# Side chains that no longer stand behind each other in the queues, and a maximum spread in float32r: a Perceiver block on one core

## The chip, the core and the metric

The kernel runs on one core of one Trainium2 chip. The metric is the device time in microseconds (us) from one launch. Three runs of the kernel before took 2706.93, 2708.26 and 2709.93 us; the median is 2708.26 us. One further execution was profiled: it took 2710.54 us, and 2708.8 us of that lie between its first and its last instruction (its span).

Five instruction streams matter. TensorE (PE) does the matmuls, with a weight load ahead of each. VectorE (DVE) and ScalarE (ACT) do elementwise work, GpSimd (POOL) as well, and SyncE (SP) issues the DMAs. Each takes its instructions in the order in which they were built into the program, so an instruction that waits holds up all behind it on its engine.

## The reference

The input is `x`, 8 batches of 64 rows by 512, and a context of 8 batches of 1601 rows by 512. Six residual blocks follow each other:

```python
x = x + L0_xattn(layernorm(x), ctx)   # 32 heads of 128, 8 key/value heads, softmax over 1601 keys
x = x + L0_attn(layernorm(x))         # Mamba: conv, selective scan over 64 steps, 1024 channels, 16 states
x = x + L0_ffn(layernorm(x))          # ternary 512 x 512
x = x + L1_xattn(layernorm(x), ctx)   # no weights: softmax(x ctx^T) ctx
x = x + L1_attn(layernorm(x))         # 32 heads of 16, rotary, causal, 64 tokens
x = x + L1_ffn(layernorm(x))          # octonion gate/up/down, ternary, hidden 1360
```

All is float32. The first block is by far the largest: keys and values are projected from the whole context for each of 8 batches and 8 key/value heads. The change touches its softmax in one place and the order of the five later blocks in another.

## The kernel before

**Attention.** `x_all` (L527) walks over 64 units, one for each batch and key/value head. A unit projects keys (`x_k`, matmuls on L363) and values (`x_v`, L334), forms scores with keys on the partitions (`x_s`, L385), copies them to SBUF (L388) and keeps a running maximum over the key tiles on DVE (L392). In the next unit's six steps the previous unit's softmax is finished: `x_max` (L397) transposes the running maximum (L403) and reduces it to one negative maximum per query, a column `mc` of 128 x 2 (L405). `x_spread` (L408) then spreads that column over all partitions: two matmuls on L412 whose stationary operand is the column broadcast to 128 x 128 and whose moving operand is the identity. DVE adds the result to the scores (L426), ACT takes the exponent (L427), POOL sums over key tiles (L429, L452), PE multiplies by the values (L464), and `x_wo` (L521) applies the output projection. Projections and scores are split in float32r high and low parts, three matmuls for each product; a float32 matmul is recorded as two.

**Side work.** While PE is occupied by the attention, other work is mixed in. `prep` (L616) splits and ternarizes the weights of the later blocks. `chain` (L779) does the five later blocks for a group of two batches: `mamba`, the small `ffn`, `xattn1`, `attn1`, `ffn1`. Groups 0 to 2 get a chain each while the attention of later batches runs; they are called chains 0, 1 and 2 here. Chain 3, for the last two batches, can only start when the attention is over, and this last stretch of the program is called the tail. All are Python generators. `run` (L1303) advances them whenever the attention yields, each at a pace set by a cost and an end (`advance`, L1331), so that prep and chain 0, chains 0 and 1, and chains 1 and 2 are in progress together for part of the time.

**Order.** A scheduler orders the traced instructions on each engine by its own timing model and the data dependences. It may move side work ahead of attention work that was traced before it. To hold it back, the chains see DVE, ACT and POOL through a wrapper (`Late`, L55; `Side`, L68). Every instruction issued through it gets an ordering edge, with no semaphore, to the instruction traced just before it on the same engine:

```python
return lambda *a, **k: self.tc.keep_in_program_order(f(*a, **k))
```

That predecessor may belong to the attention, to the same chain, or to another chain or prep. Instructions on PE and SP are not held. The wrapper is switched off (`pinning`) once the attention's last unit is traced; chain 3 is never held. In the profile all held instructions carry line L65, that of the lambda.

The four stages of the scan in `mamba` (L895) alternate between POOL, DVE, POOL and DVE. `xattn1` (L1015) streams the context again from memory for its scores (L1039) and values (L1095). In the profile, chains 0 to 2 read the context there into a tile named `b` with a left operand also named `b` (`acc<-b,b`); the rows of chain 3 name `s` in its place.

Of the kernel before, what the change touches and what calls it, by code (L numbers as in the profile page):

```python
# [9 lines left out]
FR = mybir.dt.float32r  # L10
# [6 lines left out]
P = 128  # L17
# [37 lines left out]
class Late:  # L55


    def __init__(self, kernel, eng):
        self.kernel, self.tc, self.eng = kernel, kernel.tc, eng

    def __getattr__(self, name):
        f = getattr(self.eng, name)
        if not self.kernel.pinning:
            return f
        return lambda *a, **k: self.tc.keep_in_program_order(f(*a, **k))  # L65


class Side:  # L68


    def __init__(self, kernel, engines):
        self.nc = kernel.tc.nc
        self.late = {e: Late(kernel, getattr(self.nc, e)) for e in engines}

    def __getattr__(self, name):
        return self.late.get(name) or getattr(self.nc, name)
# [2 lines left out]
class Kernel:  # L79
    def __init__(self, ctx, tc, ins, out):  # L80
        self.ctx, self.tc, self.nc = ctx, tc, tc.nc
        self.i = ins
        self.out = out
        self.B = ins["x"].shape[0] // T
        self.n = 0
        self.pinning = True
        self.flush = False

    def nm(self, s):
        self.n += 1  # L90
        return f"{s}_{self.n}"
# [55 lines left out]
    def consts(self):  # L147
        nc, i = self.nc, self.i
        c = self.ctx.enter_context(self.tc.tile_pool(name="const", bufs=1))
        self.c = c  # L150
        self.ident = c.tile([P, P], FP, name="ident")
        make_identity(nc, self.ident)
        self.eps5 = c.tile([P, 1], FP, name="eps5")
        nc.gpsimd.memset(self.eps5, 1e-5)
        self.ones = c.tile([P, P], FP, name="ones")
        nc.gpsimd.memset(self.ones, 1.0)
        self.eps6 = c.tile([P, 1], FP, name="eps6")
        nc.gpsimd.memset(self.eps6, 1e-6)

        def ld(name, shape):  # L160
            t = c.tile(shape, FP, name="c_" + name)
            nc.sync.dma_start(out=t, in_=i[name])
            return t

        self.bq = ld("bq", [P, 32])
        self.bk = ld("bk", [P, NKV])
        self.bv = ld("bv", [P, NKV])
# [229 lines left out]
    def x_max(self, b, i):  # L397

        nc = self.nc
        m = self.mf.pop((b, i))  # L400
        ps = self.px.tile([P, 2, 256], FP, name=self.nm("m_ps"), tag="m", bufs=MB)
        for h in range(2):
            nc.tensor.transpose(ps[:, 0, h * P : (h + 1) * P], m[:, 0, h * P : (h + 1) * P], self.ident)  # L403
        col = self.sb("mc", [P, 2], pool=self.xp, bufs=2)
        nc.vector.tensor_reduce(col, ps[:, 0].rearrange("p (h k) -> p h k", k=P), AX.X, ALU.max, negate=True)  # L405
        self.mm[(b, i)] = (ps, col)

    def x_spread(self, b, i):  # L408

        ps, col = self.mm[(b, i)]  # L410
        for h in range(2):
            self.nc.tensor.matmul(  # L412
                ps[:, 1, h * P : (h + 1) * P], lhsT=col[:, h : h + 1].to_broadcast([P, P]), rhs=self.ident, start=True, stop=True
            )

    def x_exp(self, b, i, n):
# [1086 lines left out]
```

## Time and profile before

| | before |
|---|---|
| median of three runs | 2708.26 us |
| profiled execution, and its span | 2710.54 us, 2708.8 us |
| PE busy | 2569.9 us, 95% |
| DVE, ACT, POOL busy | 1670.9, 1354.6, 1253.5 us |
| DMA | 455.59 MB, mean 168 GB/s |
| last attention instruction on PE ends | 2404.3 us |
| the two spread matmuls, L412 | 256 PE records, mean 283 ns |
| mean granted TensorE clock | 0.977 |

The busy times are unions of the recorded spans. PE's records overlap, since the next matmul starts while the last drains; what a matmul occupies is better read from the space between one start and the next. The chain of waits follows, from the last instruction back, what released each step.

### The profile page before, as it was taken

To read this page: it belongs to the slowest core of one execution; us is meant where nothing else is said; L and a number is where in the kernel's file an instruction comes from. 1 tells how busy PE (TensorE), PEld (TensorE's weight loads), DVE (VectorE), ACT (ScalarE), POOL (GpSimd) and SP (SyncE) were. 2 spreads that over 40 slices of the span, in tenths; PEclk is the share of its full clock that TensorE was granted. 3 is DMA by queue.
4 is the path that set the end of the run, shared out by engine and by line. 5 is a ranking of instruction groups with operands and counts; after the bars stand their busy time and mean duration, and the time that the engine had idled before them with its cause. 6 is when DMAs were issued, how large, how long until landed. Compare 5 with 4: busy or idle time off the path is not lost.

```text
span 2708.8 us, 43887 instructions
## 1 busy us (share of the span) xinstructions
PE 2569.9 (95%) x16288; PEld 2274.8 (84%) x16288; DVE 1670.9 (62%) x2723; ACT 1354.6 (50%) x3128; POOL 1253.5 (46%) x1243
## 2 busy tenths in 40 slices
PE   7999999999999899999999999999999999977787
PEld 6999999889899799978988988988898888964545
DVE  4444345577687865545577676554657777668744
ACT  4444554444566554544455545544546545446443
POOL 3212434464589864422358457521239556405410
PEclk9999999999999999999999999999999999987898
DMA  9544446665666235655234543665343454476764
GB/s 309 153 141 155 137 144 227 200 209 179 212 215 204 71 117 164 210 185 172 88 110 135 157 148 101 206 197 173 101 133 91 137 162 151 141 236 216 233 234 174
DMA packets 302934, 455.59 MB, mean 168 GB/s; under 512 B 80248, under 2 KB 179576, under 8 KB 298240
## 3 DMA queue, kind: packets, MB, share of 16 engines
q1 hardware_dynamic: 302720, 452.79, 52.2%
q8 instruction: 128, 2.10, 0.3%
q14 instruction: 86, 0.70, 0.1%
HBM read 380.23 MB, written 72.48 MB: 167 GB/s over the span
## 4 chain that ended last, share of the span: by engine, by line
PE 67%; DVE 10%; POOL 9%; DMA 7%; issue 4%; ACT 3%; SPq 0%; POOLq 0%; DVEq 0%; ACTq 0%
PE v_ps L334 15%; PE k_ps L363 15%; PE o_ps L464 10%; PE s_ps L385 8%; POOL a L65 4%; DVE a L65 3%; PE w_ps L521 3%; PE acc L274 3%; PE acc L819 2%; PE acc L1095 2%; POOL ss L452 2%; PE acc L1039 2%; PE acc L774 1%; PE acc L777 1%; DMA d_wo<-b 1%
## 5 line engine op out<-in xcount | busy, mean ns | idle before, releaser
L363 PE MATMUL k_ps<-cxb,wk 128*128 128x384 f32 x2304 | 469.9, 347 | 32.1 <-DVE mx L392 16.8
L334 PE MATMUL v_ps<-wv,cxb 128*128 128x256 f32 x3456 | 471.0, 283 | 1.4 <-DVE mx L392 1.2
L334 PEld LDWEIGHTS v_ps<-wv,cxb 128*128 128x128 f32 x3456 | 439.2, 189 | 22.0 <-issue 14.0
L363 PEld LDWEIGHTS k_ps<-cxb,wk 128*128 128x128 f32 x2304 | 405.2, 191 | 50.2 <-DVE mx L392 19.8
L464 PE MATMUL o_ps<-S,v 128*128 128x256 f32 (+1 forms) x1664 | 413.3, 381 | 6.0 <-DVE rw L479 3.9
L385 PE MATMUL s_ps<-q,kt 128*128 128x256 f32 (+1 forms) x2496 | 413.7, 299 | 5.2 <-DVE kt L109 3.1
L388 ACT COPY S<-s_ps 128x512 f32<-128x512 f32 (+1 forms) x448 | 242.4, 553 | 250.0 <-PE s_ps L385 246.9
L385 PEld LDWEIGHTS s_ps<-q,kt 128*128 128x128 f32 (+1 forms) x2496 | 342.1, 185 | 28.0 <-issue 6.9
L452 POOL TENSOR_TENSOR ss<-ss,S 128x512 f32<-128x512 f32 x254 | 353.7, 1392 | 14.6 <-ACT S L427 1.5
L429 POOL TENSOR_TENSOR ss<-S,S 128x512 f32<-128x512 f32 x64 | 85.0, 1328 | 586.9 <-ACT S L427 586.6
L392 DVE TENSOR_TENSOR mx<-s_ps,mx 128x512 f32<-128x512 f32 x256 | 175.4, 685 | 289.5 <-ACT S L388 288.8
L464 PEld LDWEIGHTS o_ps<-S,v 128*128 128x128 f32 (+1 forms) x1664 | 299.5, 190 | 45.0 <-issue 5.7
L108 ACT ACTIVATE kt<-k_ps,c_bk 128x384 fp32r<-128x384 f32 (+1 forms) x256 | 152.0, 594 | 240.7 <-PE k_ps L363 239.6
L426 DVE TENSOR_TENSOR S<-S,m_ps 128x512 f32<-128x512 f32 (+1 forms) x448 | 257.3, 641 | 24.4 <-PE m_ps L412 23.9
L427 ACT ACTIVATE S<-S 128x512 f32<-128x512 f32 (+1 forms) x448 | 247.4, 599 | 44.4 <-DVE S L426 43.8
L109 DVE SCALAR_TENSOR_TENSOR kt<-k_ps,c_bk,kt 128x384 fp32r<-128x384 f32 (+1 forms) x256 | 161.0, 629 | 170.9 <-ACT kt L108 169.4
L337 ACT COPY v<-v_ps 128x256 f32<-128x256 f32 (+1 forms) x416 | 152.7, 369 | 198.1 <-PE v_ps L334 195.7
L334 PE MATMUL v_ps<-wv,cxt 128*128 128x256 f32 (+1 forms) x1536 | 213.2, 286 | 2.7 <-DVE kt L109 1.6
L334 PEld LDWEIGHTS v_ps<-wv,cxt 128*128 128x128 f32 (+1 forms) x1536 | 195.3, 176 | 15.5 <-issue 6.5
L65 DVE TENSOR_TENSOR_SCAN a<-a,a 128x512 f32<-128x512 f32 x96 | 156.1, 1629 | 65.4 <-POOL a L65 65.4
L363 PE MATMUL k_ps<-cxt,wk 128*128 128x450 f32 x768 | 181.1, 378 | 0.9 <-DVE mx L392 0.8
L65 ACT ACTIVATE a<-lv,c_A_log 128x128 f32<-128x128 f32 x384 | 123.0, 394 | 105.3 <-DVE a L65 103.8
(358 smaller groups left out, 3971.3 us busy)
## 6 DMA issues: line engine op xcount, KB each, us to landing
wo<-d_wo SPq DMA_DIRECT2D x96, 512.0 KB, 5.0
wk<-d_wk SPq DMA_DIRECT2D x63, 512.0 KB, 3.8
wv<-d_wv SPq DMA_DIRECT2D x31, 1024.0 KB, 5.6
cst<-in_ctxT_dram SPq DMA_DIRECT2D x96, 192.0 KB, 3.1
b<-in_ctxN_dram SPq DMA_DIRECT2D x36, 512.0 KB, 3.9
d_q<-q_t SPq DMA_DIRECT2D x32, 512.0 KB, 4.4
q<-d_q SPq DMA_DIRECT2D x64, 256.0 KB, 3.5
d_wo<-b SPq DMA_DIRECT2D x32, 512.0 KB, 3.1
```

The costliest lines, as they stand in the source:

```text
L65: return lambda *a, **k: self.tc.keep_in_program_order(f(*a, **k))
L109: eng.scalar_tensor_tensor(lo, src, bias, hi.bitcast(FP), ALU.add, ALU.subtract)
L334: nc.tensor.matmul(ps[:r], lhsT=cx[:, a, c, o : o + r], rhs=w[:, m, c, :], start=k == 0, stop=k == 11)
L337: nc.scalar.copy(vt[:r], ps[:r])
L363: nc.tensor.matmul(ps[:, :wd], lhsT=w[:, a, c, :], rhs=cx[:, m, c, :], start=k == 0, stop=k == 11)
L385: nc.tensor.matmul(sp[:r, gi, :], lhsT=kt[:, a, o : o + r], rhs=q[:, m, :], start=k == 0, stop=k == 2)
L388: nc.scalar.copy(s[:r, :n], sp[:r, :n])
L392: nc.vector.tensor_tensor(mx, sp, S[0] if len(S) == 1 else mx, ALU.max)
L426: nc.vector.tensor_tensor(sv, sv, ps[:r, 1:2].to_broadcast([r, w, 256]), ALU.add)
L427: nc.scalar.activation(sv, sv, AF.Exp, scale=ISC)
L452: nc.gpsimd.tensor_tensor(ss, ss, S[n], ALU.add)
L464: nc.tensor.matmul(ps[:, 0], lhsT=self.v[(b, j, t)][:r, hc : hc + P], rhs=S[t // 2][:r, t % 2], start=t == 0, stop=t == NT - 1)
```

## The change

Two things change.

First, the wrapper gets an owner. Prep and each chain have a number, and every held instruction is noted under its number. A held instruction is now tied to the last instruction on its engine that belongs to the attention (no owner noted) or to its own chain; instructions of other chains and of prep are skipped in that search.

Second, the column `mc` becomes float32r, and the moving operand of the spread is a float32r copy of the identity, made once by ACT.

```diff
 class Late:
-    def __init__(self, kernel, eng):
-        self.kernel, self.tc, self.eng = kernel, kernel.tc, eng
+    def __init__(self, kernel, eng, own):
+        self.kernel, self.tc, self.eng, self.own = kernel, kernel.tc, eng, own
+
+    def pin(self, made):
+        owner = self.kernel.owner
+        ins = made.ins
+        for i in reversed(self.tc.nc.cur_bb.bb.instructions):
+            if i is not ins and i.engine == ins.engine and owner.get(i.name, self.own) == self.own:
+                dep = mybir.DependencyInfo(mybir.DependencyClass.NoSync, mybir.DependencyReason.DATA)
+                self.tc.add_manual_dep(ins, i.name, dep, reason="side")
+                break
+        owner[ins.name] = self.own
+        return made
 
     def __getattr__(self, name):
...
-        return lambda *a, **k: self.tc.keep_in_program_order(f(*a, **k))
+        return lambda *a, **k: self.pin(f(*a, **k))
...
 class Side:
     def __init__(self, kernel, engines):
         self.nc = kernel.tc.nc
-        self.late = {e: Late(kernel, getattr(self.nc, e)) for e in engines}
+        kernel.sides += 1
+        self.late = {e: Late(kernel, getattr(self.nc, e), kernel.sides) for e in engines}
...
+        self.sides, self.owner = 0, {}
...
+        self.ident_r = c.tile([P, P], FR, name="ident_r")
+        nc.scalar.copy(self.ident_r, self.ident)
...
-        col = self.sb("mc", [P, 2], pool=self.xp, bufs=2)
+        col = self.sb("mc", [P, 2], FR, pool=self.xp, bufs=2)
...
-                ps[:, 1, h * P : (h + 1) * P], lhsT=col[:, h : h + 1].to_broadcast([P, P]), rhs=self.ident, start=True, stop=True
+                ps[:, 1, h * P : (h + 1) * P], lhsT=col[:, h : h + 1].to_broadcast([P, P]), rhs=self.ident_r, start=True, stop=True
```

## The prediction

> **What bounds the kernel now.** I read the page first, then stretches of the span, the groups of instructions, the chain of waits in order of time, and the timeline around one spread.
>
> ```profile
> span 2708.8 us, 43887 instructions
> PE 2569.9 (95%) x16288; PEld 2274.8 (84%) x16288; DVE 1670.9 (62%) x2723; ACT 1354.6 (50%) x3128; POOL 1253.5 (46%) x1243
> PE   7999999999999899999999999999999999977787
> PEclk9999999999999999999999999999999999987898
> ```
>
> PE is busy throughout, except for the last five of 40 slices: the tail, from 2404 to 2709 us. Stretches show where PE still idles under the attention, and which engine is then loaded (the columns: length, then PE, weight loads, DVE, ACT and POOL busy, granted clock, DMA share, GB/s):
>
> ```profile
> 1400.00:1500.00 100.00, 98.01 (x681) 87.62 (x679) 74.64 (x111) 56.35 (x134) 72.09 (x70) 1.00 0.41 121
> 2100.00:2200.00 100.00, 97.08 (x621) 89.92 (x620) 73.01 (x106) 51.30 (x126) 53.30 (x57) 0.99 0.45 140
> 2200.00:2300.00 100.00, 94.10 (x595) 85.90 (x593) 73.53 (x94) 51.42 (x131) 63.10 (x70) 1.00 0.51 162
> 2300.00:2404.00 104.00, 93.44 (x561) 84.53 (x562) 64.49 (x111) 45.28 (x109) 36.67 (x37) 0.95 0.45 147
> 2404.00:2553.00 149.00, 114.81 (x670) 81.14 (x668) 119.37 (x217) 85.44 (x251) 65.30 (x73) 0.82 0.69 224
> 2553.00:2709.00 156.00, 129.18 (x660) 75.65 (x660) 75.26 (x150) 54.65 (x120) 22.71 (x23) 0.90 0.66 225
> ```
>
> From 100 to 2404 us PE idles only some 61 us in all. So PE work added under the attention is paid nearly in full, and PE work saved there is won. In the tail, to 2553 us, DVE is the dense one (119 of 149 us: chain 3's scan). After that nothing is, and latency decides.
>
> What fills the tail beside chain 3 is the rest of chain 2. The chain of waits passes through it:
>
> ```profile
> 2451.63 1.93 PE acc L1095 x4
> 2453.57 6.50 DMA b<-in_ctxN_dram
> 2460.11 3.71 PE acc L1095 x8
> 2463.83 4.93 DMA b<-in_ctxN_dram
> 2468.80 3.68 PE acc L1095 x6
> ```
>
> These are chain 2's value matmuls (chain 3's own come at 2594 us). I gave every record of the trace its chain, by lining the records up with the built program. From 2404 us on, the chain of waits is 183 us chain 3, 74 us chain 2, 29 us DMA, the rest issue and unassigned.
>
> **The change, part by part.** The sum is made against the profiled execution, 2710.5 us, which is 2.2 us above the median of the runs, 2708.3.
>
> *The spread.* The group, and one spread in the timeline:
>
> ```profile
> L412 PE MATMUL m_ps<-ident,mc 128*128 128x128 f32 x256 | 41.1, 283 | 5.9 <-DVE mc L405 5.8
> 1364.72 0.53 PEld L412 LDWEIGHTS m_ps<-ident,mc 128*128 128x128 f32 x4
> 1364.84 0.60 PE L412 MATMUL m_ps<-ident,mc 128*128 128x128 f32 x4
> 1367.88 3.00 PE L334 MATMUL v_ps<-wv,cxt 128*128 128x256 f32 x24
> ```
>
> Two matmuls make four records, 64 times. From one PE start to the next they occupy 25.4 us in all (99 ns each). In float32r there is one record for each matmul, 128 in all. No float32r row has a moving operand under 256 columns, so the price is bounded. At worst a 128-column matmul still takes what two records take: gain 0. At best it takes half the spacing of L334 (24 in 3.00 us, about 118 ns for 256 columns), some 59 ns: 128 x 59 ns = 7.5 us, gain 17.9 us. I take one record's spacing, half of 25.4: ordinary 128-column weight loads follow each other no closer than about 108 ns anywhere in the trace (here 4 in 0.53 us, of which the last lasts 0.19: 113 ns). **Gain 12 us**, ends 0 and 18.
>
> The Trainium skill, "FP8 and Floating Point Precision", TensorE Precision Notes, has true FP32 as four passes; by that alone a quarter would remain, and the gain would be 19 us. "TensorE: Matmul & The Clock Gate", LDWEIGHTS, puts a load at its columns over 1.2 GHz, 107 ns for 128, which would stop the gain at half. The spacing above sides with the second.
>
> The copy of the identity lies in ACT's wait for its first DMA (6.49 us from 2.01 us on); without that cover it costs some 0.3 us, like other copies of 128 columns. The reduction L405 has the same shape. Both at nothing.
>
> *The order.* Read from the two built programs. Prep and chain 0 barely move. Chains 1 and 2, no longer tied to their predecessors' late stages, move up. On the clock of the attention's own instructions, chain 2's last mamba projection moves from 2369 to 2235 us. Of chain 2's 434 PE instructions, 320 stood behind the last attention matmul; now 201 do. Its `ffn` and all of its `xattn1` go under the attention, between 2211 and 2394 us of that clock, with their context loads in SP's queue; `attn1` and `ffn1` stay in the tail. Three costs follow.
>
> (a) PE under the attention. The same two blocks of chains 0 and 1 occupy PE there for 31.5 and 31.7 us, start to start; in the tail chain 2's take 62 us, waits for DMA included. From 2200 to 2404 us PE idles 5.9 + 10.6 = 16.5 us, of which I let a third be filled. **Loss 26 us**; ends 15 (all idle filled) and 62 (the waits come along; the row above at 147 GB/s against 224 in the tail speaks against it).
>
> (b) Denser scans. The mambas of chains 1 and 2 take fewer attention instructions. With the recorded durations in the new order, DVE's load in 100 us of the attention's clock rises from 82 to 95 us (1400 to 1500), from 73 to 86 (2000 to 2100) and from 78 to 95 (2100 to 2200); no stretch held over 86 before. It falls at 1600 and 2200, where PE idled 10 and 5.9 us. DVE's records hold up `kt` and the maximum that free PSUM for the next key and score matmuls. I take 4 us for each of the three and half of one back: **loss 8 us**. Ends: a gain of 16 (the relieved idle goes, none comes) and a loss of 30 (10 us each, as in the worst stretch of before, 1600 to 1700).
>
> A rule speaks against the change here. "SBUF — State Buffer", two separate sides, lets a DVE instruction with two SBUF inputs and a GpSimd one that reads SBUF exclude each other. The scan's multiply L953 on DVE takes 1413 ns with two SBUF inputs, L957 with one in PSUM 680 ns, which agrees but doesn't separate the causes; by the rule the loss would lie near its upper end.
>
> (c) The tail, 305 us. To the end of chain 3's mamba (2553 us), chain 2's DVE work beside it is 19.9 us before and 20.2 after (`attn1` for `xattn1`); as DVE is dense, little is won: 5 us. From there on chain 2's share falls: in chain 3's `ffn` 7.8 us of recorded PE time before and 7.7 after, in `xattn1` 18.0 and 13.3, in `attn1` 26.8 and 7.0, in `ffn1` 16.9 and 0. Its parts of the chain of waits there are 11.7 + 5.8 (a weight load), 4.7, 16.6 and 12.2 us. Scaled by these ratios, and half of the load, they lose 0.2 + 2.9, 1.2, 12.3 and 12.2: 29 us. What comes second then shows, so I take 25: **gain 30 us** with the 5. Ends 10 (chain 3's own latencies behind) and 60 (all but a third of chain 2's and the DMA's 103 us).
>
> Sum: -12 + 26 + 8 - 30 = **-8 us**: 2702.5 in a profiled execution, and against the median **2700 us**.
>
> **The rivals.**
>
> *DVE crowding decides (slower).* In the three dense stretches DVE is loaded to 86-95%, it stands in order, and PE idles 10 us in each, as at 1600 before: (b) is 30, the sum +14, 2722 us. For it: in 50 us pieces the load above 90% rises from 6 to 26 us. Against: from 800 to 900 us DVE at 75 and POOL at 92 us left PE idle only 7.7. It decides from (b) above 16 us.
>
> *Float32r gains nothing at 128 columns.* The sum is +4, 2712 us. For it: no such row exists. Against: one record instead of two is what all float32r rows show.
>
> *The tail shrinks to chain 3 alone.* Chain 3's own 183 us, 16 us of issue and unassigned, 29 of DMA and a fifth of chain 2's 74: some 245, a gain of 60 and a sum of -38, 2670 us. For it: chain 2 leaves the last two blocks almost wholly. Against: DVE bounds the scan.
>
> That the order doesn't change is excluded by the built programs; whether the hardware keeps pace with it is what (a) and (b) price.
>
> **How the numbers follow.** The forecast, 2688 to 2714 us, has 0.42; crowding 0.27; no float32r gain 0.17; the short tail 0.14. About 0.2%, 5.4 us, is what can be told from no change: faster is below 2703, slower above 2713.7. Faster: 0.27 of the forecast, 0.14, and 0.05 of the third case: 0.46. Slower: 0.03, 0.25 and 0.03: 0.31. Within: 0.23. The range is 2674 to 2732 us: it reaches nearly to the short tail, and ten above the crowded case, as (a) may add to it.
>
> **What would show it.** L412 with 128 records and spacings near 108 ns; chain 2's L1039 and L1095 (`acc<-b,b`) done before the last L521; attention ending on PE near 2426 us (2404 - 12 + 26 + 8); the tail some 275 us long. Wrong would be: an attention that ends after 2445 us, PE waits for `b<-in_ctxN_dram` in the middle of the attention's last units, or a tail still of 300 us because chain 3's own latencies fill it.

## The result, and the profile after

The changed kernel takes 2723.44 us (median of 4 runs, 2718.50 to 2724.91) against 2707.60 us of the kernel before on the same chip: a ratio of 1.0057, 95% interval 1.0039 to 1.0075. It is slower by 16 us; the forecast was 2700 us. The profiled execution took 2724.91 us, 14.4 us more than the one of before.

Lines of the changed kernel stand 11 to 15 higher: L427 was L412, L1277 was L1262. The page:

```profile
span 2723.1 us, 43692 instructions
...
PE 2552.8 (94%) x16160; PEld 2259.5 (83%) x16160; DVE 1687.8 (62%) x2723; ACT 1352.2 (50%) x3129; POOL 1245.1 (46%) x1243
...
PE   7999999999999999999998999999998999985686
...
PEclk9999999999999999999999999999999999997888
```

PE has 128 records fewer, as the float32r spread should have. The attention's last matmul ends at 2426.8 us (before 2404.3; forecast 2426), so the attention is 22.5 us longer and the tail 296.3 us for 304.5 (forecast 275). The same stretches as before the change (length, then PE, weight loads, DVE, ACT, POOL busy, granted clock, DMA share, GB/s):

```profile
1400.00:1500.00 100.00, 89.34 (x592) 79.70 (x592) 87.31 (x118) 61.73 (x155) 79.97 (x84) 0.98 0.38 118
...
1600.00:1700.00 100.00, 100.00 (x665) 95.00 (x664) 62.21 (x95) 49.82 (x118) 44.50 (x47) 1.00 0.47 158
...
2000.00:2100.00 100.00, 92.40 (x624) 80.86 (x623) 85.98 (x112) 58.39 (x149) 89.26 (x90) 1.00 0.40 125
2100.00:2200.00 100.00, 93.84 (x585) 86.40 (x584) 80.41 (x106) 57.21 (x142) 70.78 (x75) 0.98 0.42 132
2200.00:2300.00 100.00, 100.00 (x664) 94.54 (x663) 56.77 (x102) 45.49 (x107) 30.60 (x27) 1.00 0.52 172
2300.00:2427.00 127.00, 123.62 (x750) 95.20 (x749) 58.60 (x112) 50.65 (x112) 21.06 (x22) 0.99 0.58 186
2427.00:2573.00 146.00, 96.60 (x599) 75.34 (x599) 121.58 (x215) 80.66 (x234) 76.75 (x83) 0.80 0.55 189
2573.00:2723.00 150.00, 110.05 (x530) 65.12 (x529) 60.10 (x119) 46.83 (x101) 10.47 (x12) 0.86 0.55 186
```

Two of these stretches before the change:

```profile
1600.00:1700.00 100.00, 89.98 (x549) 83.40 (x548) 71.91 (x97) 50.50 (x135) 67.21 (x77) 0.95 0.34 109
...
2000.00:2100.00 100.00, 97.67 (x655) 85.46 (x654) 66.98 (x108) 58.34 (x134) 71.98 (x70) 0.99 0.34 103
```

From 1400 to 1500 us PE, which was at 98, falls to 89 while DVE rises from 75 to 87. From 1600 to 1700 us it goes the other way: PE rises from 90 to 100 and DVE falls from 72 to 62. From 2200 us on PE is full, with chain 2's two blocks in it. But chain 3's mamba still needs 146 us after the attention, and the rest 150 us (146 and 158 before). The spread:

```profile
L427 PE MATMUL m_ps<-ident_r,mc 128*128 128x128 f32 x128 | 24.9, 270 | 4.0 <-DVE mc L420 4.0
```

```profile
1370.32 0.30 PEld L427 LDWEIGHTS m_ps<-ident_r,mc 128*128 128x128 f32 x2
1370.43 0.33 PE L427 MATMUL m_ps<-ident_r,mc 128*128 128x128 f32 x2
```

From one PE start to the next the spread occupies 15.8 us for 25.4: 9.6 us are won. The chain of waits in the tail, by the owner of each step, is 188 us chain 3 (183 before), 47 us chain 2 (74), 22 us DMA (29), 36 us issue and unassigned (16). What chain 2 gave up was hardly won.

In start-to-start times, each with the idle time behind it and cut at the attention's end, the whole difference is: spread -9.6; other matmuls of the attention 2043.6 to 2051.2, +7.6; side work under the attention 325.6 to 350.0, +24.4; tail -8.2. Together +14.2 us; the two spans differ by 14.3.

### The profile page after: what moved, and what is told of

Its sections match the earlier page's. It is cut to its first block, busy times and chain, and to the rows that moved or that the text cites. A ratio compares the mean times of both kernels' runs of the same rounds, so it can differ in the third digit from the quotient of the medians.

```text
span 2723.1 us, 43692 instructions
## 1 busy us (share of the span) xinstructions
PE 2552.8 (94%) x16160; PEld 2259.5 (83%) x16160; DVE 1687.8 (62%) x2723; ACT 1352.2 (50%) x3129; POOL 1245.1 (46%) x1243
## 4 chain that ended last, share of the span: by engine, by line
PE 65%; DVE 13%; POOL 9%; DMA 6%; issue 4%; ACT 2%; SPq 1%; POOLq 0%; DVEq 0%; ACTq 0%
PE v_ps L349 15%; PE k_ps L378 14%; PE o_ps L479 9%; PE s_ps L400 8%; POOL a L76 4%; DVE a L76 3%; PE w_ps L536 3%; PE acc L289 3%; PE acc L1110 2%; PE acc L1054 2%; POOL ss L467 2%; PE acc L834 2%; DVE b L76 1%; PE acc L789 1%; PE acc L792 1%
## 5 line engine op out<-in xcount | busy, mean ns | idle before, releaser
L76 POOL TENSOR_TENSOR a<-a,bc 128x512 f32<-128x512 f32 x96 | 128.5, 1339 | 91.0 <-DVE a L76 88.3
```

The source lines that it names most:

```text
L76: return lambda *a, **k: self.pin(f(*a, **k))
```

## Experiments

"Attention" is the end of the attention's last matmul on PE, "tail" what follows, both from the one profiled execution. Ratios are to the kernel before, with their intervals. They were measured on several chips (the kernel before took 2707.6 us in the comparison above and 2713.4 us in those below), so ratios are compared rather than times, and a difference of 5 us between the attention ends of two profiles means little.

### The two parts alone

The spread alone, in the kernel before:

```diff
+        self.ident_r = c.tile([P, P], FR, name="ident_r")
+        nc.scalar.copy(self.ident_r, self.ident)
-        col = self.sb("mc", [P, 2], pool=self.xp, bufs=2)
+        col = self.sb("mc", [P, 2], FR, pool=self.xp, bufs=2)
-   ... rhs=self.ident, ...
+   ... rhs=self.ident_r, ...
```

> The kernel before with the spread in float32r alone; every held instruction is still tied to the one traced just before it. If the two parts add up and the spread is worth what its own records say (the two matmuls occupied 25.4 us from start to start before and 15.8 after, both under the attention, where PE is nearly always busy): 2707.6 - 9.6 = 2698 us. If the spread gains nothing in the whole kernel: 2707 us. A third possibility: the built program places chain 2 a little later (20 of the 109 recorded-in-order PE instructions of its mamba now stand behind the last attention matmul, none before); if that decides, the tail grows beyond 305 us and the time is 2705 to 2715 us.

Measured: 2733.70 us, **1.0075** (1.0062 to 1.0088). The attention ends at 2394.5 us, 9.8 earlier. That this is the 9.6 us of the spread is chance: by the start-to-start times the spread occupies 8.5 us less here (16.9 us), the attention's other matmuls 7.6 more, and the side work up to that point 9.0 less, since part of chain 2 has fallen behind it. The tail is 338.8 us, 34 longer. The third possibility is what happened, with a larger loss than the 2705 to 2715 us named. Changing one operand's type makes the scheduler lay out all engines anew, and chain 2 falls behind on the attention's clock. PE after the attention in this kernel:

```profile
2394.32 1.05 PE L821 MATMUL acc<-a,a 128*128 128x128 f32 x8
...
2403.81 0.79 PE L776 MATMUL acc<-w,a 128*128 128x512 f32 x1 [6.09 <-ACT a L65]
...
2407.79 0.80 PE L778 MATMUL acc<-w,a 128*128 128x512 f32 x1 [1.90 <-DMA w<-d_wout]
...
2411.44 0.79 PE L778 MATMUL acc<-w,a 128*128 128x512 f32 x1 [1.96 <-DMA w<-d_wout]
...
2422.63 2.72 PE L821 MATMUL acc<-a,w 128*128 128x128 f32 x11
```

The first four are chain 2's last gate projections (`acc<-a,a`) and output projections, each waiting for its own inputs; chain 3's first projections (`acc<-a,w`) stand behind them, 28 us after the attention's end for 5 before.

The order alone (the changed kernel with the three lines above undone):

> The changed kernel with the spread back in float32: the order alone. If the two parts add up: 2722.6 + 9.6 = 2732 us, with an attention that ends on PE near 2436 us and a tail of 296 us. If the spread was worth nothing: 2723 us. If the order by itself was a gain and the two parts hurt each other: below 2708 us.

Measured: 2731.79 us, **1.0071** (1.0055 to 1.0086); attention 2447.7, tail 282.4 us. Each part alone loses some 19 us and both together 16: they don't add up. (The 2732 us forecast was met only because the kernel before also took 2713.4 us on this chip; the attention and the tail were both off, by 12 and 14 us.) The spread pushes chain 2 back, the order pulls it forward. Why this tail is 14 us shorter than the changed kernel's with almost the same instructions in it was not found; chain 3's scan ends 139.5 us after the attention for 146.4, and the stretch behind it takes 22.5 us for 29.2.

### What chain 2's ffn and xattn1 cost, in the tail and under the attention

Both blocks are left out for group 2 and their paces handed back, so that the rest keeps its place:

```diff
+            if gi == 2 and k in (1, 2):
+                yield from paced(x, None if k == 1 else x)
+                continue
```

> The kernel before without chain 2's ffn and xattn1 (left out, with the same paces handed back, so the output of chain 2's two batches lacks these two blocks). In the kernel before they stand in the tail. Forecast of the prediction, term (c): without them the tail falls from 305 to about 275 us and the time to 2678 us. Theory now: the tail is chain 3's own chain of latencies, and chain 2's steps only stood where chain 3 waited anyway; the tail falls by no more than the 9 us seen after the change, to 296, and the time is 2696 to 2703 us.

> The changed kernel without chain 2's ffn and xattn1 (left out in the same way). In the changed kernel they stand under the attention. If they are paid there as PE time (33.6 us from start to start, some of it in idle): the attention ends 26 to 34 us earlier, near 2395 to 2400 us, the tail stays 296 us, and the time is 2690 to 2697 us. If they were free there and the dense scans are what costs: the attention ends near 2420 us and the time stays above 2712 us.

Measured, in the kernel before: 2692.42 us, 0.9921 (0.9905 to 0.9937), attention 2407.0, tail 283.9 us. In the changed kernel: 2694.00 us, 0.9927 (0.9913 to 0.9941), attention 2395.0, tail 292.2 us. Under the attention the blocks cost 31.8 us, as forecast. In the tail of before they cost 20.6 us: less than my 30, but more than the 9 that the new theory allowed, so that theory falls in its simple form. What counts is not only how much of chain 2 is gone, but what is put in its place.

### What is left in the changed tail

Chain 2's attn1 and ffn1 left out of the changed kernel (`blocks[: 3 if gi == 2 else LAST_STAGE - 1]`), and then its ffn1 alone (`4 if`):

> The changed kernel without chain 2's attn1 and ffn1, which are all of chain 2 that stands in its tail (left out, so the output of chain 2's two batches is that of its xattn1). The tail then holds chain 3 alone. The prediction's rival of a short tail, and its reading of the chain of waits (47 us of the changed kernel's tail are chain 2's instructions): tail 245 to 255 us, time 2672 to 2682 us. Theory now (chain 3's own latencies fill those places): the tail falls only from 296 to 280 or so, the attention ends as in the changed kernel, time 2705 to 2715 us.

> The changed kernel without chain 2's ffn1 alone (left out, so the output of chain 2's two batches is that of its attn1); its attn1 still stands in the tail. With attn1 and ffn1 both left out the scan of chain 3 ended 128 us after the attention, with both 146, and 17 and 30 us passed from there to chain 3's xattn1. Theory: the 18 us in the scan are chain 2's attn1, whose DVE work stands in the same queue as chain 3's scan; the 13 us after it are ffn1. So here the scan still ends near 146 us, xattn1 begins 17 us later, and the tail is 282 to 285 us, the time 2708 to 2714 us. Rival: any work of chain 2 at all costs the whole, tail 293 or more; or attn1 is free and ffn1 is the whole cost, scan end 128 to 132, tail 265 to 270 us.

Measured: 2693.64 us, 0.9921 (0.9907 to 0.9934), attention 2428.7, tail 264.4 us; and 2706.91 us, 0.9978 (0.9969 to 0.9987), attention 2429.6, tail 279.7 us. The empty tail came out between the two forecasts (280 and 245 to 255): chain 3's latencies are most of it, but company costs more than the theory had it. The split between the two blocks came out as expected, the tail 2 us shorter. I cut each tail at chain 3's own records: end of its scan matmuls, start and end of its xattn1, start of the up and gate matmuls of its ffn1. Stretches of the kernel before, the changed one, the one without ffn1, and the one with chain 3 alone:

```profile
2404.00:2550.00 146.00, 113.14 (x661) 80.02 (x660) 117.94 (x213) 83.95 (x249) 64.84 (x72) 0.81 0.68 221
2550.00:2580.00 30.00, 22.35 (x86) 11.49 (x86) 16.29 (x32) 8.40 (x19) 10.89 (x11) 0.82 0.95 330
...
2611.00:2676.00 65.00, 53.90 (x252) 29.31 (x251) 30.50 (x62) 22.00 (x45) 8.10 (x9) 0.92 0.74 255
2676.00:2708.80 32.80, 23.61 (x102) 18.48 (x100) 13.50 (x26) 12.11 (x24) 0.00 (x0) 0.90 0.18 60
```

```profile
2427.00:2573.00 146.00, 96.60 (x599) 75.34 (x599) 121.58 (x215) 80.66 (x234) 76.75 (x83) 0.80 0.55 189
2573.00:2603.00 30.00, 18.05 (x74) 13.52 (x75) 14.08 (x28) 9.40 (x19) 2.74 (x4) 0.82 0.85 284
...
2634.00:2692.00 58.00, 39.47 (x171) 18.23 (x172) 23.33 (x48) 15.58 (x33) 7.73 (x8) 0.88 0.47 163
2692.00:2723.00 31.00, 21.54 (x81) 16.27 (x79) 10.69 (x19) 9.84 (x18) 0.00 (x0) 0.78 0.06 20
```

```profile
2430.00:2574.00 144.00, 96.30 (x599) 75.06 (x599) 120.43 (x209) 80.26 (x232) 78.31 (x80) 0.81 0.52 174
2574.00:2591.00 17.00, 7.41 (x22) 4.42 (x21) 6.70 (x17) 2.46 (x7) 2.60 (x3) 0.73 0.84 260
...
2621.00:2677.00 56.00, 37.12 (x153) 15.09 (x154) 19.69 (x41) 12.72 (x28) 7.72 (x8) 0.82 0.50 164
```

```profile
2429.00:2557.00 128.00, 73.14 (x442) 66.39 (x443) 103.41 (x176) 70.58 (x211) 63.49 (x68) 0.73 0.39 128
2557.00:2574.00 17.00, 7.89 (x22) 4.53 (x20) 6.65 (x17) 2.46 (x7) 2.61 (x3) 0.66 0.82 259
...
2605.00:2661.00 56.00, 36.81 (x152) 14.90 (x152) 19.48 (x40) 13.08 (x28) 7.73 (x8) 0.82 0.48 164
2661.00:2693.00 32.00, 22.51 (x81) 17.13 (x81) 11.38 (x20) 9.84 (x18) 0.00 (x0) 0.77 0.06 19
```

(xattn1, 30 to 31 us in all four, is left out of the fences.) The reader sees three things. Chain 3's ffn1 takes some 32 us with or without company, its attn1 56 to 58 us with little or none and 65 with chain 2's blocks beside it. The stretch between scan and xattn1 takes 17 us with chain 2 absent or with its attn1 only, 30 us when chain 2's ffn1 (changed) or attn1 (before) stands there. And the scan takes 128 us alone, 144 to 146 us with either block beside it. In all four the scan's length is DVE's busy time plus 24 to 28 us: leaving out attn1 took 17.0 us from DVE and 16 from the stretch. That attn1 beside the scan costs 15 us of tail (279.7 to 264.4) and ffn1 17 (296.3 to 279.7) is shown, by one profile each (the ratios of the medians give 15 and 21 us, give or take 5); that DVE is the reason for the first is argued from this equality, since leaving out attn1 also takes work from PE, ACT and POOL away.

So the change moved `ffn` and `xattn1` out of the tail, and `attn1` and `ffn1` moved up beside the scan and chain 3's ffn, where they cost the same. Nothing was won up to chain 3's xattn1 (176 us after the attention in both); behind it 7 us in attn1 and under 1 in ffn1 (by the records' own times 64.6 to 57.4 and 32.4 to 31.8 us; the windows above are cut at whole microseconds).

### The blocks put back behind the attention

One number of the changed kernel, chain 2's pace, is enough for it (`SPAN` sets for each chain over how much of the attention its work is spread; a larger number is a slower pace):

```diff
-SPAN = [3.1,3.1,2.6,0.2]
+SPAN = [3.1,3.1,3.4,0.2]
```

> The changed kernel with chain 2's pace 3.4 for 2.6: in the built program chain 2's ffn and xattn1 stand behind the last attention matmul again, as before the change, and its mamba ends 1 attention unit ahead of the end (3 in the changed kernel); chain 1 stays where the change put it. Theory: what the change lost is that two blocks went under the attention, where they cost some 32 us of PE, and the tail gave back only 9; so here the attention ends near 2397 us, the tail is 295 to 305 us, and the time is 2695 to 2703 us. Rival (the denser scans under the attention are what costs): chain 1's dense stretch is still there, the attention ends above 2405 us and the time is 2708 to 2716 us.

Measured: 2703.28 us, **0.9952** (0.9939 to 0.9964), attention 2399.8, tail 302.0 us. The whole loss turns into a gain of 10 us: the attention is 27 us shorter than in the changed kernel, the tail 6 us longer. The rival, with 2708 us and more, is out as the main cause.

The same with the spread in float32:

> The changed kernel with chain 2's pace 3.4 and the spread back in float32; in the built program every block stands on the attention's clock as with the spread in float32r at that pace. Theory: the spread is worth what its records say where the order stays the same, 9.6 us: ratio to the kernel before about 1.000 (0.9952 with float32r at this pace), attention end near 2409 us. Rival: the spread is worth nothing and the gain of that kernel is the order's alone: ratio near 0.995.

Measured: 2707.56 us, 0.9976 (0.9967 to 0.9985), attention 2411.6, tail 296.7 us. That is midway between the theory (1.000) and its rival (0.995): the spread is worth 0.24%, some 6.5 us, with an uncertainty of about 4; its records say 27.0 us for 15.5. It is worth something, but no more than its records. The order is fixed only in the built program: as measured, the attention's other matmuls take 9.6 us less here than with float32r at that pace and the side work 10.2 us more.

### Which chain's freedom costs

`Late` gets its owner from a table: `(1, 1, 3, 3)[kernel.sides - 1]` leaves chain 1 free of chain 0 and ties chain 2 to chain 1; `(1, 1, 1, 4)` frees chain 2 alone.

> The changed kernel, but prep and chain 0 share one owner and chains 1 and 2 share the other: chain 1 is free of chain 0, chain 2 is tied to chain 1 as before. In the built program chain 1 stands as in the changed kernel, chain 2's mamba ends at unit 62.6 of 64 (63.6 before, 59.9 changed), its ffn and 16 of the 56 score matmuls of its xattn1 stand under the attention, the rest behind. Theory (the blocks under the attention are the cost): attention ends near 2402 us, tail 295 to 305 us, time 2700 to 2706 us. Rival (freeing chain 1 is what costs, through its dense scan at 1400 to 1500 us): 2713 to 2722 us.

> The changed kernel, but prep, chain 0 and chain 1 share one owner and chain 2 has its own: chain 1 tied to chain 0 as before, chain 2 free of chain 1. In the built program chain 2's mamba ends at unit 61.9 of 64, its ffn and half of the score matmuls of xattn1 stand under the attention; chain 1 stands as with the spread alone. Theory: cost under the attention in proportion (ffn and a quarter to a half of xattn1, 10 to 16 us), tail 295 to 303 us, ratio to the kernel before 0.996 to 1.001. Rival (denser scans decide, and chain 2's alone remains): attention end above 2415 us, ratio above 1.003.

Measured: chain 1 free 2702.28 us, **0.9956** (0.9941 to 0.9970), attention 2401.9, tail 303.3 us. Chain 2 free 2716.52 us, **1.0012** (1.0003 to 1.0021), attention 2414.2, tail 301.6 us. With chain 1 free PE still idles 12.6 us from 1400 to 1500 us, and yet the kernel is faster than before; from 1600 to 1700 us, where PE idled 10 us before, it is now full. With chain 2 free the ratio is just above what the theory allows and the attention ends a little under the rival's bound: half of xattn1 lies under the attention, and from 2100 to 2200 us, where DVE is at 81, PE idles 12.3 us. Both causes act there, and by the start-to-start times the dense stretch is the larger: the attention's other matmuls take 12.5 us more than in the kernel before, the side work 6.4 us more.

### The spread alone, with chain 2 a little sooner

The spread alone, with the pace 2.5 for chain 2 (`SPAN = [3.1,3.1,2.5,0.2]`):

> The float32r spread alone with chain 2's pace 2.5 for 2.6: in the built program the last mamba projection of chain 2 stands before the last attention matmul again (in the spread alone 8 of 64 stood behind it). Theory: the 34 us that the spread alone lost in the tail (339 for 305) come from those few instructions, behind which chain 3's first projections wait (28 us after the attention's end for 5); with them back under the attention the tail is 300 to 310 us, the attention ends near 2395 to 2400 us and the time is 2698 to 2704 us. Rival: the spread loses by itself, through its own column or the new order of the attention: the time stays above 2725 us.

Measured: 2715.80 us, 1.0008 (0.9999 to 1.0017), attention 2387.9, tail 325.6 us. The rival is out, and 18 of the 20 us lost come back, but the theory's tail doesn't. Chain 3 starts in time now (7 us after the attention) and its ffn1 begins at 260 us, sooner than before (272); but chain 2's own ffn1 (`w_r,b_r`) runs until the end and ends last. Of the groups in the last 24 us:

```profile
L776 PE MATMUL acc<-w_r,b_r 128*128 128x512 f32 x7 | 4.7, 676 | 1.2 <-ACT b_r L105 1.2
...
L776 PE MATMUL acc<-w_r,b_r 128*128 128x336 f32 x8 | 2.8, 350 | 0.6 <-ACT b L1268 0.6
```

So chain 2 can be too late in two ways: ahead of chain 3 in the queues, or behind it at the end.

### Less dense scans as well

```diff
-SPAN = [3.1,3.1,2.6,0.2]
+SPAN = [3.1,3.3,3.4,0.2]
```

> The changed kernel with the paces 3.3 for chain 1 and 3.4 for chain 2 (3.1 and 2.6): chain 2's blocks stand as in the kernel with 3.4 alone, and chain 1's mamba takes 12.9 attention units for 12.1, so its scan is less dense. Theory (blocks under the attention decide, density little): ratio to the kernel before 0.993 to 0.996, within 3 us of the kernel with 3.4 alone (0.9952). If density matters, PE idles less than 11 us from 1400 to 1500 us and the ratio is 0.990 to 0.993.

Measured: 2685.90 us, **0.9901** (0.9888 to 0.9914), attention 2393.0, tail 295.3 us: 27 us faster than the kernel before, the fastest of all that computed the whole result. The theory missed: the ratio lies below its range and inside that of the other case, and PE idles 7.2 us from 1400 to 1500 us, under the 11 named for it. So the density of the scans counts too, beside the blocks under the attention. With the pace 3.4 alone and then with both:

```profile
1400.00:1500.00 100.00, 88.84 (x594) 79.74 (x594) 87.61 (x119) 62.22 (x156) 81.71 (x84) 0.98 0.40 118
2000.00:2100.00 100.00, 89.95 (x581) 80.40 (x580) 86.89 (x112) 55.27 (x138) 76.88 (x80) 0.95 0.37 116
```

```profile
1400.00:1500.00 100.00, 92.78 (x604) 82.98 (x602) 86.03 (x118) 60.29 (x152) 78.68 (x81) 0.97 0.37 115
2000.00:2100.00 100.00, 99.19 (x666) 86.08 (x666) 73.74 (x114) 60.04 (x145) 75.33 (x75) 1.00 0.43 133
```

The larger step is from 2000 to 2100 us, in chain 2's scan: DVE drops from 87 to 74 us and PE's idle time from 10 to 1. That scan starts sooner and is spread further (its scan instructions on DVE start between 1965 and 2284 us, for 2005 and 2288), and 7 of its 32 stand in this stretch for 11. Chain 1's attn1 stands beside it in both. Under the attention PE idles 64.7 us for 71.5, and the attention is 6.8 us shorter. The further 6.7 us in the tail lie mostly in chain 3's attn1 (62.9 us for 73.8) and were not traced to a cause.

## Why the prediction was wrong

The sum was -12 + 26 + 8 - 30; measured by the same steps it is -9.6 + 24.4 + 7.6 - 8.2.

- **Spread, 12 us: a little large.** 9.6 us. The step that took half of 25.4 us assumed that one record keeps its spacing of 99 ns; it became 123 ns (15.8 us over 128). The loads of a pair do follow each other by some 113 ns, as the prediction had it, but its two matmuls start 59 ns apart.
- **(a), 26 us: right.** 24.4 us more side work, and 31.8 and 27.0 us when the blocks were left out or put back. Of PE's idle time from 2200 us on more was filled than a third: 16.5 us before, 3.4 after. By these steps a part of that relief is counted under (b).
- **(b), 8 us: the number came out, partly by luck.** The attention's own matmuls take 7.6 us more, but that is a balance of larger parts. PE idles 8.7 us more from 1400 to 1500 us and 8.5 more from 2000 to 2200 us, where 4 us were put for each of three stretches, and 10.0 and 5.9 us less from 1600 to 1700 and from 2200 to 2300 us, of which 4 were counted. The spread alone, with the old order, also shows 7.6 us more. So these dense stretches and their relief are shown, but not that they are the 7.6 us. The rival of crowding came out at nearly the right time, 2722 us, but not by its mechanism: it needed 30 us here. Nor did the loss lie near its upper end, as the prediction took it from the rule of the Trainium skill's "SBUF — State Buffer", two separate sides, on two SBUF inputs; no run separated that rule from other causes.
- **(c), 30 us: wrong, and it decides the sign.** 8.2 us. "Scaled by these ratios", chain 2's steps in the chain of waits were to vanish with chain 2's PE time, 12.3 us in attn1 and 12.2 in ffn1. They gave 7.2 and 0.6. Chain 3's ffn1 takes 32 us even alone: what chain 2's instructions held on that chain, chain 3's own waits and its own matmuls, recorded as longer (last section), fill again. And the 4.3 us from ffn and xattn1 and the 5 from the scan were none, since chain 2's next blocks moved up into the freed places. The floor, put at 245 us, is 264: even a tail with chain 3 alone gives back 40 us, not 60. (The end of 60 was itself mis-added: two thirds of 103 us are 69.)

The warning stood in the prediction ("a tail still of 300 us because chain 3's own latencies fill it"), but no case with a chance of its own was made of it. Of the marks, 128 records, `acc<-b,b` under the attention and an attention that ends at 2426.8 us were met; spacings near 108 ns and a tail of 275 us were not. The attention's end rests on the same luck as (b).

## What to carry to other kernels

Work moved from a stretch that latency bounds to one that PE fills is paid nearly in full where it goes and won only in part where it leaves: price what comes second, the critical chain alone on its own, before counting the removed work's steps on the chain of waits, and ask what moves up into its place. When a scheduler orders by a timing model, any edit, even one operand's type, moves everything; look in the built program at where the side work falls against the main work's clock, and retune the paces before judging the edit. Here the change cost 16 us at the old paces and, together with two new ones, saved 27; the kernel before was not run at other paces, so how much of the 27 the paces alone would have saved is open.

## What was not expected of the hardware

- A float32r matmul with a moving operand of 128 columns is one record, and the two of a pair start 59 ns apart (median of 59 such pairs). The Trainium skill, "TensorE: Matmul & The Clock Gate", "Wait — 56ns, not 53.3ns?", gives 55.6 ns for back-to-back matmuls of 128 columns at full clock, without naming float32r; the 59 ns are close to it. Yet the spread occupies 123 ns for each record, because the next matmul starts late, 112 ns (median) after the second; the two loads of a pair follow each other by some 110 ns (0.30 us for both, the last lasting 0.19).
- With less work beside the critical chain TensorE was granted a lower clock. In the last stretch the granted clock is 0.90 before, 0.78 after and 0.77 with chain 3 alone, and chain 3's ffn1 matmuls add up to 37.1 us of recorded time for 33.5 before. This was not tested by itself; it may be one of the ways in which a tail gives back what it wins.
